# A graph layer on one core: where the first node numbers lie, and when the counts are taken

## The chip, the core and the metric

The kernel runs on one core of a Trainium2 chip. The metric is the device time of one execution in microseconds; the median of three runs is given. The engines have short names in all that follows: PE is TensorE (matmuls; PEld are its weight loads), DVE is VectorE, ACT is ScalarE, POOL is GpSimd, SP is SyncE. SBUF is the on-chip memory that all engines and DMAs reach; PSUM is the memory that PE writes its results to.

## The reference

There are 6250 nodes with 64 features and 206250 edges with 64 features each. Cut to what matters:

```python
msg = concatenate([x[dst], edge_attr], axis=1)        # 128 wide, one row per edge
h = relu(msg @ W1a.T + b1a) @ W1b.T + b1b             # the edge MLP, 128 hidden
sums, counts = segment_sum(h, src), segment_sum(ones, src)   # by the node src
agg = sums / maximum(counts, 1)
z = relu(concatenate([x, agg]) @ W2a.T + b2a) @ W2b.T + b2b  # the node MLP
y = concatenate([z, x]) @ Wr.T + br
out = layernorm(x + y)
```

The edges come sorted by dst. They have to be summed by src, which is in no order.

## The kernel before, in words

The host pads the edges and sends them in 124 blocks of 13 tiles of 128 edges (1664 edges a block). The blocks are taken in a fixed scattered order. A second, general path runs only where the data breaks the fast path's assumptions; it does not run here. All line numbers are those of the profile.

For each block k, the fast path does these steps.

- **Loads** (`group`, L1148 to L1170): SP issues the edge features of the block, transposed, and what names the dst nodes. Since the edges are sorted by dst, a block only meets 64 neighbouring nodes, its window. The first 8 blocks (NEAR) load their dst list and the 64 nodes; later ones load ready-made places in the window and rows of a table.
- **Columns** (`columns`, L1172): a one-hot of each edge's node within its window, so that one matmul handles both the edge and its node. For the first 8 blocks DVE makes it at L1184, comparing the dst list with `near_f`, which holds the window's node number for each of 64 partitions. For later blocks ACT makes it, in two passes (L1179, L1181).
- **Window** (`window`, L1189): for the first 8 blocks, a matmul (L1192) of the 64 nodes with the first layer's weights, and a copy by ACT (L1193) into `mv`, the weights of that block.
- **First layer** (`hidden`, L1199): 13 tiles, one matmul each in two passes (L1206), in groups of 4, 3, 3 and 3 that share a PSUM tile; ACT applies the relu (L1209) into the block's row tile `orow`, of which there are five.
- **Bins and counts**: src divided by 128 gives an edge's bin (49 of them). `carried` (L943) copies the running count of the block before into a first column (ACT, L956 or L959; DVE, L952, in the first blocks). `bins_of` (L915) makes one-hots by bin (L930) and scans them (L936), on DVE. `counts_of` (L963) turns them into each edge's rank in its bin with matmuls over partitions (L972, L973, L975), into the one PSUM tile `cnt`. `slots` (L978) reads `cnt` on DVE (L993 and, through `quads`, up to L1059) and writes the row index of every edge. Since there is one `cnt`, the counts of a block wait until the slots of the block before have read it.
- **Joins** (blocks 5 to 103): six or three of the tiles are added up by node into groups of four rows before they are written (marks by DVE at L1092, matmuls at L1115).
- **Scatter** (L1211): POOL issues one indirect DMA for each tile that is left (L1245) and for each joined group (L1217): 1306 in all. They write rows into tables in DRAM, sorted by bin. Some of them are told to wait for first-layer tiles, joins or sums of the block two places later.
- **Sums**: rows of bins that are full are read back (SP), DVE makes one-hots of their nodes (L1333), PE adds them up (L1352) and DVE or ACT adds the result to `part`.

Behind the last block come the sums of what is left and the node MLP with the norm (L1626 to L1690).

What sets the order: PE, ACT, DVE and SP run their instructions in the order in which the program writes them (a manual schedule). POOL's order is set by the framework's scheduler, which takes the instructions that are ready first by its own planning. Each engine takes its instructions strictly in order and waits on semaphores.

The main loop (L1501) prepares ahead: iteration k runs the first layer of block k, the counts and slots of block k + 1, the columns, the carried column and the scan of block k + 2, and the loads of block k + 3. Ahead of the loop (L1494 to L1500), block 0's window matmul, carried column, scan, counts, columns and slots run in the order written there.

`near_f` is 8 columns of `cnt` itself, in a PSUM bank that the counts also use: `cnt[:, 1, 448 : 456]`.

Of the kernel before, what the change touches and what calls it, by code (L numbers as in the profile page):

```python
# [8 lines left out]
F32 = mybir.dt.float32  # L9
# [8 lines left out]
P = 128  # L18
# [434 lines left out]
NEAR = 8  # L453
# [29 lines left out]
def fast_path(  # L483
# [61 lines left out]
    def joined(k):  # L545
        if not JOIN_FROM <= k < JOIN_TO:
            return 0
        return 2 if TWICE_FROM <= k < TWICE_TO else 1

    def direct(k):  # L550
        return BLK - JOIN * joined(k)
# [98 lines left out]
    const = ctx.enter_context(tc.tile_pool(name="fconst", bufs=1))  # L650
# [91 lines left out]
    with (  # L742
# [80 lines left out]
        def starts_at(joints):  # L823


            if joints:
                d = BLK - JOIN * joints
                nc.vector.memset(words, 1.0 + 0x3F80 * 2.0**-23)
                v = words.rearrange("p (b t) -> p b t", t=TJ)
                for c in (0, d + 1, TJ, TJ + d + 1):  # L830
                    if c % 2 == 0:
                        nc.vector.memset(v[:, :, c // 2], 1.0)
                    else:
                        nc.vector.memset(v.bitcast(I32)[:, :, c // 2], 0x3F80)
            else:
                v = words[:, : HALF * T]
                nc.vector.memset(v, 1.0 + 0x3F80 * 2.0**-23)
                nc.vector.memset(v.rearrange("p (b t) -> p b t", t=T // 2)[:, :, 0], 1.0)
# [9 lines left out]
        bins(0, HEAD)  # L848

        cnt = slpp.tile([P, 2, 512], F32, name="cnt_ps")  # L850
        near_f = cnt[:, 1, 448 : 448 + NEAR]
        z_ps = steady[:, P + 2 + HALF * TJ :][:, : 2 * JOIN]
        of_first = cnt[:, :, HALF * TJ : HALF * TJ + HALF]
        assert T % 2 == 0 and TJ % 2 == 1
# [60 lines left out]
        def bins_of(k):  # L915


            ep_ = epoch_of[k]
            c0 = k * BLK
            oh = ohs.pop(k)  # L920
            if joined(k) != joined(k - 1):
                starts_at(joined(k))
            t = TJ if joined(k) else T
            had = slp.tile([P, 2 * HALF * t], BF16, name="had", padded_shape=[P, 2 * HALF * TJ])
            by_bin = oh.rearrange("p (b t) -> p b t", t=t)
            d = direct(k)
            for t0, c, n in ((1, c0 + BLK - d, d), (d + 2, c0, BLK - d)):
                if n == 0:
                    continue
                nc.vector.tensor_tensor(  # L930
                    by_bin[:, :, t0 : t0 + n],
                    ramp[:, : 2 * HALF, None].to_broadcast([P, 2 * HALF, n]),
                    hi[:, None, c : c + n].to_broadcast([P, 2 * HALF, n]),
                    op=ALU.is_equal,
                )
            nc.vector.tensor_tensor_scan(had, on[:, : 2 * HALF * t], oh, 0.0, op0=ALU.mult, op1=ALU.add)  # L936
            oh, had = (v.rearrange("p (b t) -> p b t", t=t) for v in (oh, had))
            hads[k] = had
            return oh, had
# [3 lines left out]
        def carried(k):  # L943


            t, d = (TJ if joined(k) else T), direct(k)
            oh = ohs[k] = slp.tile([P, 2 * HALF * t], BF16, name="bins", padded_shape=[P, 2 * HALF * TJ])
            by_bin = oh.rearrange("p (b t) -> p b t", t=t)
            if k == epoch_of[k].first:
                nc.vector.memset(by_bin[:, :, 0], 0.0)  # L950
            elif k < JOIN_FROM:
                nc.vector.tensor_tensor(  # L952
                    by_bin[:, :, 0], hads[k - 1][:, :, BLK], ramp[:, 1:2].to_broadcast([P, 2 * HALF]), op=ALU.mult
                )
            elif joined(k) and joined(k - 1) == joined(k):
                nc.scalar.copy(by_bin[:, :, 0 : d + 2 : d + 1], hads[k - 1][:, :, d : d + 2])  # L956
                return
            else:
                nc.scalar.copy(by_bin[:, :, 0], hads[k - 1][:, :, direct(k - 1)])  # L959
            if joined(k):  # L960
                nc.scalar.copy(by_bin[:, :, d + 1], none_b)

        def counts_of(k, oh, had):  # L963
            t = oh.shape[2]

            ps = cnt
            for i in range(2):
                v = ps[:, i, : HALF * t].rearrange("p (b t) -> p b t", t=t)  # L970
                b = slice(i * HALF, (i + 1) * HALF)
                nc.tensor.matmul(v, one_w, had[:, b, :], start=True, stop=False)  # L972
                nc.tensor.matmul(v[:, :, : t - 1], before_w, oh[:, b, 1:], start=False, stop=True)  # L973
                if joined(k) == 2:
                    nc.tensor.matmul(of_first[:, i, :], one_w, had[:, b, direct(k) + 1 + JOIN], start=True, stop=True)  # L975
            return ps
# [171 lines left out]
        def group(g):  # L1148

            rhs = rhss[g % EDGES]  # L1150
            if g < NEAR:
                all_of = dst[g * NG * P : (g + 1) * NG * P].rearrange("(o e) -> o e", o=1)
                s = nc.sync.dma_start(rhs[D:, :].bitcast(I32), all_of.to_broadcast([WIN, NG * P]))
                edges(g)
                with tc.issue_after(s.ins):
                    w = nc.sync.value_load(win_i[0:1, g : g + 1], min_val=0, max_val=N - WIN)
                nc.sync.dma_start(near[:D, g, :], xT[:, bass.ds(w, WIN)])
                return rhs, None, mv[g % MV]
            edges(g)

            half = NG * P // 2
            rel = rhs[D:, :].bitcast(BF16).rearrange("p (h e) -> p h e", h=2)[:, :, half:]
            s = nc.sync.dma_start(
                rel, relt[g : g + 1, :].rearrange("o (h e) -> o h e", h=2).to_broadcast([WIN, 2, half])
            )
            with tc.issue_after(s.ins):
                w = nc.sync.value_load(win_i[0:1, g : g + 1], min_val=0, max_val=N - WIN)
            m = mv[g % MV]
            nc.sync.dma_start(m[D:, :], ytab[bass.ds(w, WIN), :])
            return rhs, rel, m  # L1170

        def columns(g, part_of=0):  # L1172


            rhs, rel, _ = made[g]
            if g >= NEAR:
                of_win = rhs[D:, :].rearrange("p (h e) -> p h e", h=2)
                if part_of == 0:
                    nc.scalar.activation(of_win, rel, AF.Square, bias=from_win[D:, :])  # L1179
                else:  # L1180
                    nc.scalar.activation(rhs[D:, :], rhs[D:, :], AF.Relu, bias=ones[D:, :1], scale=-1.0)  # L1181
                return
            if part_of == 0:
                nc.vector.tensor_tensor(  # L1184
                    rhs[D:, :], rhs[D:, :].bitcast(I32), near_f[D:, g : g + 1].to_broadcast([WIN, NG * P]),
                    op=ALU.is_equal,
                )

        def window(g):  # L1189

            ps = hp.tile([P, H], F32, name="h_ps")
            nc.tensor.matmul(ps[D:, :], near[: D + 1, g, :], w1x_t, start=True, stop=True)  # L1192
            nc.scalar.copy(mv[g % MV][D:, :], ps[D:, :])  # L1193
# [5 lines left out]
        def hidden(k, parts):  # L1199
            orow = orows[k % ROWS]  # L1200
            rhs, _, m = made[k]
            for k0, n in parts:
                ps = hp.tile([P, SUB, H], F32, name="h_ps")
                for j in range(n):
                    c = k0 + j
                    done[k, c] = nc.tensor.matmul(  # L1206
                        ps[:, j, :], rhs[:, c * P : (c + 1) * P], m, start=True, stop=True
                    ).ins.name
                nc.scalar.activation(orow[:, k0 : k0 + n, :H], ps[:, :n, :], AF.Relu)  # L1209
# [283 lines left out]
        )  # L1493
        for g in range(3):  # L1494
            made[g] = group(g)
        window(0)
        carried(0)
        counts = counts_of(0, *bins_of(0))
        columns(0)
        slots(0, counts)  # L1500
        for k, ep_ in enumerate(epoch_of):  # L1501
# [15 lines left out]
            if k == 0:  # L1517
                hidden(k, ((0, 4), (4, 3), (7, 3), (10, 3)))
                window(1)
                columns(1)  # L1520
                carried(1)
                ahead = bins_of(1)
            if k + 1 < NGR:
                counts = counts_of(k + 1, *ahead)
            if k + 2 < NGR:
                carried(k + 2)
            if k > 0:
                hidden(k, ((0, 4), (4, 3), (7, 3)))
            if k + 2 < NEAR:
                window(k + 2)  # L1530
            if k == NEAR - 6:
# [255 lines left out]
```

## Time and profile before

| | us |
|---|---|
| three runs | 1740.62, 1749.65, 1750.46 |
| their median | 1749.65 |
| the profiled execution | 1742.9 |
| its span, first to last instruction | 1741.1 |
| PE busy | 1495.1 (86%) |
| DVE busy | 1451.1 (83%) |
| POOL busy | 1255.2 (72%) |
| ACT busy | 900.1 (52%) |
| mean granted PE clock | 0.953 |

A row of a group reads: line, engine, operation, what it writes and reads, number of instructions; then busy time in us and the mean of one in ns; then the engine's idle time just before these instructions, and what ended most of it. "issue" is idle time in which the engine waited for nothing that the profile shows. A row of the timeline reads: start and length in us, engine and line; equal neighbours are merged (x26), and the brackets tell the idle time before. SPq, ACTq and POOLq are the sequencers, which issue DMAs. All durations come from one profiled execution.

### The profile page before, as it was taken

Reading aid. Unit: us, or ns where it says so; the run is one execution under the profiler, and the core shown is the slowest. Engines: PE = TensorE matmul, PEld = TensorE weight load, DVE = VectorE, ACT = ScalarE, POOL = GpSimd, SP = SyncE. Lnnn points to the kernel's source line nnn. Section 1 sums busy time; section 2 is a strip of 40 time slices with the busy share of each in tenths; the row PEclk is TensorE's granted clock in tenths of the full one; section 3 lists DMA queues with packets and bytes.
Section 4 is the critical chain, followed back from the end, with each engine's and each line's share of the span. In section 5 each row is a group of like instructions: output and inputs, shape, how many; then the busy total and the mean of one; then the engine's idle time right before and its main releaser. Section 6 shows DMA issues by size and latency. Waiting matters only on the chain. (4 is left out here: it accounts for less than half of the span.)

```text
span 1741.1 us, 36105 instructions
## 1 busy us (share of the span) xinstructions
PE 1495.1 (86%) x12229; PEld 1426.3 (82%) x12229; DVE 1451.1 (83%) x3408; ACT 900.1 (52%) x1797; POOL 1255.2 (72%) x1323
## 2 busy tenths in 40 slices
PE   5668888888888888776899999989889999999987
PEld 4568878788878787766798999889889898999976
DVE  8489999999999899766788988989877676888777
ACT  2257777666766666554555555545443333443026
POOL 5777777777777777777777777777777777777720
PEclk9789999989999999978999999999999999999998
DMA  8878888856666565558799999879788888999971
GB/s 185 217 242 273 275 271 271 278 175 190 189 189 189 169 200 169 163 167 238 213 267 271 288 286 276 272 233 269 221 248 255 247 239 252 273 322 298 334 231 47
DMA packets 216190, 408.89 MB, mean 235 GB/s; under 512 B 43265, under 2 KB 122740, under 8 KB 215868
## 3 DMA queue, kind: packets, MB, share of 16 engines
q1 hardware_dynamic: 127770, 230.22, 47.1%
q0 software_dynamic: 49136, 117.56, 20.7%
q10 hardware_dynamic: 39090, 58.69, 10.6%
q8 instruction: 100, 1.64, 0.4%
q14 instruction: 94, 0.77, 0.1%
HBM read 228.29 MB, written 178.01 MB: 233 GB/s over the span
## 5 line engine op out<-in xcount | busy, mean ns | idle before, releaser
L1245 POOL DMA_INDIRECT rows<-orow,rowidx x1153 | 1105.8, 959 | 368.6 <-issue 216.0
L1352 PE MATMUL h_ps<-rt,oh 128*128 128x129 f32 x4202 | 511.4, 280 | 44.8 <-DVE oh L1333 17.4
L1352 PEld LDWEIGHTS h_ps<-rt,oh 128*128 128x128 f32 x4202 | 495.1, 196 | 50.6 <-issue 21.6
L1206 PE MATMUL h_ps<-mv,rhs 128*128 128x128 f32 x3224 | 416.2, 285 | 26.3 <-ACT orow L1209 18.4
L1206 PEld LDWEIGHTS h_ps<-mv,rhs 128*128 128x128 f32 x3224 | 397.5, 200 | 38.8 <-ACT orow L1209 21.3
L1209 ACT ACTIVATE orow<-h_ps 128x512 f32<-128x512 f32 x496 | 255.1, 538 | 302.8 <-PE h_ps L1206 296.2
L1333 DVE TENSOR_TENSOR oh<-ramp,rt 128x512 f32<-128x512 f32 (+4 forms) x466 | 332.3, 752 | 26.9 <-DMA rt<-rows 22.3
L1115 PE MATMUL h_ps<-orow,shared 128*128 128x130 f32 (+1 forms) x2376 | 302.6, 285 | 38.9 <-ACT orow L1209 32.6
L1115 PEld LDWEIGHTS h_ps<-orow,shared 128*128 128x128 f32 x2376 | 291.7, 200 | 43.3 <-ACT orow L1209 37.0
L936 DVE TENSOR_TENSOR_SCAN had<-ramp,bins 128x750 bf16<-128x750 bf16 (+1 forms) x124 | 210.6, 1699 | 99.0 <-ACT bins L956 90.3
L1179 ACT ACTIVATE rhs<-rhs,from_win 64x1664 f32<-64x1664 bf16 x116 | 194.6, 1677 | 2.9
L1181 ACT ACTIVATE rhs<-rhs,ones 64x1664 f32<-64x1664 f32 x116 | 194.6, 1677 | 2.9
L1092 DVE TENSOR_TENSOR shared<-quad_ramp,ramp 128x1536 f32<-128x1536 f32 x99 | 173.4, 1751 | 11.0 <-PE h_ps L1115 4.8
L1507 ACT CAST orow<-lo 128x13 f32<-128x13 bf16 x124 | 26.5, 214 | 292.9 <-DMA rows<-orow,rowidx 256.9
L972 PE MATMUL cnt_ps<-had,one_w 128*128 128x375 bf16 (+1 forms) x248 | 81.8, 332 | 85.5 <-DVE at_q L1059 74.0
L1115 PE MATMUL h_ps<-orow,oh 128*128 128x130 f32 (+1 forms) x1296 | 154.3, 275 | 0.0
L1115 PEld LDWEIGHTS h_ps<-orow,oh 128*128 128x128 f32 x1296 | 149.8, 190 | 0.0
L1119 ACT COPY shared<-h_ps 128x260 f32<-128x260 f32 x168 | 62.2, 378 | 109.2 <-PE h_ps L1115 51.1
L930 DVE TENSOR_TENSOR bins<-ramp,hi 128x300 bf16<-128x300 f32 (+2 forms) x223 | 113.7, 548 | 0.3
L1409 DVE TENSOR_TENSOR part<-part,h_ps 128x387 f32<-128x387 f32 (+2 forms) x207 | 89.9, 435 | 21.2 <-PE h_ps L1352 20.4
L973 PEld LDWEIGHTS <-before_w 128*128 128x128 bf16 x248 | 25.5, 103 | 99.9 <-issue 94.3
L1217 POOL DMA_INDIRECT quads<-shared,qidx x84 | 80.6, 960 | 25.6 <-issue 10.7
(161 smaller groups left out, 1291.9 us busy)
## 6 DMA issues: line engine op xcount, KB each, us to landing
rhs<-in_edgeT SPq DMA_DIRECT2D x124, 416.0 KB
rt<-rows SPq DMA_DIRECT2D x106, 390.0 KB
rt<-rows SPq DMA_DIRECT2D x145, 260.0 KB
rt<-quads SPq DMA_DIRECT2D x97, 260.0 KB
rhs<-relt SPq DMA_DIRECT2D x116, 208.0 KB
rows<-padrow ACTq DMA_DIRECT2D x12, 1560.0 KB
rows<-orow,rowidx POOLq DMA_INDIRECT x1153
rt<-rows SPq DMA_DIRECT2D x48, 325.0 KB
```

The source lines that it names most:

```text
L930: nc.vector.tensor_tensor(by_bin[:, :, t0 : t0 + n], ramp[:, : 2 * HALF, None].to_broadcast([P, 2 * HALF, n]), hi[:, None, c : c + n].to_b ...
L936: nc.vector.tensor_tensor_scan(had, on[:, : 2 * HALF * t], oh, 0.0, op0=ALU.mult, op1=ALU.add)
L1092: nc.vector.tensor_tensor(m, quad_ramp.rearrange("p g q -> p (g q)")[:, None, :].to_broadcast([P, JOIN, QUAD * P]), z_ps[:, i * JOIN : (i ...
L1115: done[k, f"join{i}"] = nc.tensor.matmul(ps[:, j, :w], m[:, t, (g0 + j) * P : (g0 + j + 1) * P], orow[:, i * JOIN + t, :w], start=t == 0, ...
L1179: nc.scalar.activation(of_win, rel, AF.Square, bias=from_win[D:, :])
L1181: nc.scalar.activation(rhs[D:, :], rhs[D:, :], AF.Relu, bias=ones[D:, :1], scale=-1.0)
L1206: done[k, c] = nc.tensor.matmul(ps[:, j, :], rhs[:, c * P : (c + 1) * P], m, start=True, stop=True).ins.name
L1209: nc.scalar.activation(orow[:, k0 : k0 + n, :H], ps[:, :n, :], AF.Relu)
L1245: s = nc.gpsimd.indirect_dma_start(out=ep_.rows, out_offset=bass.IndirectOffsetOnAxis(ap=rowidx[:, k % RING * BLK + j : k % RING * BLK + j ...
L1333: nc.vector.tensor_tensor(res[:, at_tile : at_tile + nb * n, :], ramp[:, None, :].to_broadcast([P, nb * n, P]), node[:, :, None].to_broadc ...
L1352: m = nc.tensor.matmul(of_bin(b), oh[:, at_tile, :], rt[:, j * n + t, : H + 1], start=t0 + t == st.lo[b], stop=t0 + t == st.hi[b] - 1,)
L1409: nc.vector.tensor_add(to, to, g.ps[:, : g.nb, :])
```

## The change

Three things. First, `near_f` becomes a small tile of its own in SBUF, instead of columns of the counts' PSUM tile. Second, ahead of the loop the counts of block 0 come before the window matmul of block 0 on PE, and before the window's copy on ACT. Third, in every iteration from block 1 on, the first group of four first-layer tiles of block k (matmuls and relu) comes ahead of the counts of block k + 1 and ahead of the carried column of block k + 2; the next two groups stay where they were.

```diff
-        near_f = cnt[:, 1, 448 : 448 + NEAR]
+        near_f = const.tile([P, NEAR], F32, name="near_f")
...
         for g in range(3):
             made[g] = group(g)
-        window(0)
         carried(0)
         counts = counts_of(0, *bins_of(0))
+        window(0)
         columns(0)
         slots(0, counts)
...
+            if k > 0:
+                hidden(k, ((0, 4),))
             if k + 1 < NGR:
                 counts = counts_of(k + 1, *ahead)
             if k + 2 < NGR:
                 carried(k + 2)
             if k > 0:
-                hidden(k, ((0, 4), (4, 3), (7, 3)))
+                hidden(k, ((4, 3), (7, 3)))
             if k + 2 < NEAR:
                 window(k + 2)
```

## The prediction

> **What bounds the kernel now.** I read four views in this order: engine totals, the windows by stage, the groups, and the timeline of the first 20 us. The totals (busy time, share of the span, instructions) come first.
>
> ```profile
> span 1741.1 us, 36105 instructions
> PE 1495.1 (86%) x12229; PEld 1426.3 (82%) x12229; DVE 1451.1 (83%) x3408; ACT 900.1 (52%) x1797; POOL 1255.2 (72%) x1323
> ```
>
> By these shares TensorE looks like the bound, and POOL like a bystander. The windows view, cut at the first and the last scatter, says otherwise (columns: length, then busy time and instruction count of each engine, granted clock, DMA share, GB/s).
>
> ```profile
> 0.00:17.10 17.10, 5.49 (x23) 4.30 (x24) 11.28 (x29) 2.84 (x6) 2.51 (x17) 1.00 0.86 179
> 17.10:1671.10 1654.00, 1436.70 (x11828) 1375.64 (x11828) 1389.85 (x3237) 858.26 (x1610) 1252.68 (x1306) 0.96 0.81 240
> 1671.10:1741.10 70.00, 52.91 (x383) 46.32 (x381) 49.95 (x144) 39.02 (x182) 0.00 (x0) 0.88 0.41 120
> ```
>
> All 1306 scatters lie in the middle stage. 1654.0 / 1306 = 1.266 us for each. Is that a fixed pace, or POOL waiting for others? The groups and the last scatters answer it.
>
> ```profile
> L1245 POOL DMA_INDIRECT rows<-orow,rowidx x1153 | 1105.8, 959 | 368.6 <-issue 216.0 <-DMA rows<-orow,rowidx 45.2 <-PE h_ps L1206 22.7
> L1217 POOL DMA_INDIRECT quads<-shared,qidx x84 | 80.6, 960 | 25.6 <-issue 10.7 <-DMA rows<-orow,rowidx 4.0 <-DVE oh L1333 1.8
> L1217 POOL DMA_INDIRECT quads<-rt,qidx x69 | 66.3, 961 | 21.0 <-issue 11.9 <-DMA rows<-orow,rowidx 2.1 <-DVE hit_q L1139 1.5
> ...
> 1668.84 0.96 POOL L1245 DMA_INDIRECT rows<-orow,rowidx  x1 [0.30 <-issue]
> 1670.10 0.96 POOL L1245 DMA_INDIRECT rows<-orow,rowidx  x1 [0.30 <-issue]
> ```
>
> Three groups, one duration (959 to 961 ns), and 0.30 us before each even where nothing is waited for. 1305 gaps of 0.30 are 391.5 us. The idle time of the groups is 368.6 + 25.6 + 21.0 = 415.2, of which 13.95 lie before the first scatter (below), so 401.3: some 10 us at most are true waiting in 1654. The hundreds in between say the same, where TensorE idles and where it doesn't:
>
> ```profile
> 400.00:500.00 100.00, 86.04 (x730) 82.00 (x729) 95.02 (x254) 68.37 (x137) 75.91 (x80) 0.98 0.63 190
> ...
> 700.00:800.00 100.00, 65.98 (x455) 61.83 (x454) 66.80 (x179) 51.30 (x98) 75.75 (x80) 0.83 0.59 167
> ...
> 1500.00:1600.00 100.00, 100.00 (x888) 98.83 (x888) 86.62 (x132) 43.72 (x58) 75.89 (x80) 1.00 1.00 313
> ```
>
> Eighty scatters start in each, whatever PE and DVE do. So the span is **17.1 us to the first scatter + 1654.0 of scatters back to back + 70.0 behind the last**. An edit counts only if it moves the first scatter, stalls POOL, or touches the tail.
>
> **The change part by part.** *The start.* These rows of the timeline (start, length, engine, line; in brackets the idle time before and what ended it) carry it:
>
> ```profile
> 2.16 0.58 SPq L1153 DMA_DIRECT2D rhs<-in_dst_o  x1
> 4.76 0.50 SPq L1157 DMA_DIRECT2D rt<-in_xT  x1
> 6.47 1.62 DVE L936 TENSOR_TENSOR_SCAN had<-ramp,bins 128x700 bf16<-128x700 bf16 x1
> 9.59 0.66 PE L1192 MATMUL h_ps<-w1x_t,rt 65*64 65x128 f32 x2 [9.59 <-DMA rt<-in_xT]
> 10.18 0.47 PE L972 MATMUL cnt_ps<-had,one_w 128*128 128x350 bf16 x1
> 10.28 0.26 ACT L1193 COPY mv<-h_ps 64x128 f32<-64x128 f32 x1 [5.91 <-PE h_ps L1192]
> 11.03 0.50 PE L973 MATMUL cnt_ps<-bins,before_w 128*128 128x325 bf16 x1
> 11.56 1.89 DVE L1184 TENSOR_TENSOR rhs<-rhs,cnt_ps 64x1664 f32<-64x1664 int32 x1 [3.47 <-PE cnt_ps L973]
> 13.55 5.37 PE L1206 MATMUL h_ps<-mv,rhs 128*128 128x128 f32 x26 [2.03 <-issue]
> 14.59 0.17 DVE L1000 SCALAR_TENSOR_TENSOR rowidx<-row,bin_at 128x13 int32<-128x13 f32 x1
> 15.63 0.60 ACT L1209 ACTIVATE orow<-h_ps 128x512 f32<-128x512 f32 x1 [4.85 <-PE h_ps L1206]
> 17.10 1.13 POOL L1245 DMA_INDIRECT rows<-orow,rowidx  x1 [13.95 <-DVE rhs L1184]
> ```
>
> Now: the one-hots of block 0 (L1184) read near_f out of the tile of the counts and wait 3.47 us for the last count; the first layer starts 0.1 us after they end at 13.45; the first scatter is issued 17.10 - 13.55 = 3.55 us later. After the change near_f is a tile of its own, and in the compiled order the first L1184 waits only for its load. It can start at the scan's end, 6.47 + 1.62 = 8.09, and end at 9.98. The counts run from 8.1: four matmuls that now take 10.18 to 11.53 end at about 9.5. The window matmul still waits for its load until 9.59 and its copy ends at 10.54. So the first layer starts at about 10.6, not 13.55. The new row indices end 9.98 + (14.76 - 13.45) = 11.3, early enough. **First scatter: 10.6 + 3.55 = 14.15, 2.95 us earlier.** The second L1184, which the page names as releaser, ends by 13.2 and doesn't hold it.
>
> The one unknown is when the list that L1184 reads has landed. It was issued at 2.16, 2.6 us ahead of a load that was there at 9.59. If it lands at 8.09 or before, the gain is 2.95. If at 9.59, L1184 ends at 11.48, the first layer starts at 11.58, and the gain is 1.97. I take 2.95: the earlier issue is the nearer row.
>
> L1184 itself changes an operand from PSUM to SBUF. No row has that operation with both operands in SBUF, so I compare two other tensor-tensor rows of one size:
>
> ```profile
> L1679 DVE TENSOR_TENSOR normed<-y,rstd 128x192 f32<-128x192 f32 (+1 forms) x17 | 6.0, 350 | 0.5
> L1665 DVE TENSOR_TENSOR y<-h_ps,xr 128x192 f32<-128x192 f32 (+1 forms) x17 | 5.8, 341 | 0.4 <-PE h_ps L1663 0.4
> ```
>
> SBUF with SBUF took 350 ns, PSUM with SBUF 341: 3% either way, 0.06 us on 1.89, eight times. Nothing.
>
> *The counts behind four tiles.* TensorE's wait ahead of the counts goes:
>
> ```profile
> L972 PE MATMUL cnt_ps<-had,one_w 128*128 128x375 bf16 (+1 forms) x248 | 81.8, 332 | 85.5 <-DVE at_q L1059 74.0 <-DVE row L993 7.8 <-DVE early L998 3.4
> ```
>
> That is 85.2 us over 123 blocks, 0.69 each, which four tiles fill: 8 passes of 3.15 / 26 = 0.12 us make 0.97 us. Since POOL sets the pace it is worth 0 at the end. What it may cost is seen in a block of the stage where DVE is fullest:
>
> ```profile
> 296.50 0.30 DVE L1059 TENSOR_TENSOR at_q<-cnt_ps,second 128x150 f32<-128x150 f32 x1
> 296.85 0.32 PE L972 MATMUL cnt_ps<-had,one_w 128*128 128x375 bf16 x1 [1.77 <-DVE at_q L1059]
> 297.57 3.15 PE L1206 MATMUL h_ps<-mv,rhs 128*128 128x128 f32 x26
> 299.17 0.60 ACT L956 COPY bins<-had 128x100 bf16<-128x100 bf16 x1
> 299.36 0.84 ACT L1209 ACTIVATE orow<-h_ps 128x512 f32<-128x512 f32 x1
> 301.97 1.72 DVE L936 TENSOR_TENSOR_SCAN had<-ramp,bins 128x750 bf16<-128x750 bf16 x1
> 304.48 0.51 DVE L993 TENSOR_REDUCE row<-cnt_ps 128x7 f32<-128x350 f32 x1
> 307.47 0.30 DVE L1059 TENSOR_TENSOR at_q<-cnt_ps,second 128x150 f32<-128x150 f32 x1
> ```
>
> Two things come later. The counts come up to 0.97 us later where PE wasn't waiting; their reader (L993) starts at 304.48, 6.7 us after they end at 297.75. The carried column (L956) now queues on ACT behind the activation of the four tiles, 0.60 us as at 15.63; the scan that needs it starts 2.2 us after its end at 299.77. Both are covered. Without the cover the price would be 0.97 + 0.60 = 1.57 us of DVE a block. Behind the copy on ACT stand the other activations, whose work is the same. No DMA is moved in any queue's order; SP's loads for later blocks wait for first-layer tiles of earlier ones, which come no later.
>
> *Stalls and the tail.* The only long wait between scatters, and the longest issue on ACT's queue, lie in the stage that loads and writes most:
>
> ```profile
> 90.91 0.97 POOL L1245 DMA_INDIRECT rows<-orow,rowidx  x1 [2.52 <-issue]
> 51.85 17.74 ACTq L807 DMA_DIRECT2D ytab<-part  x1
> ```
>
> If transfers there keep their own time while POOL comes 2.95 us earlier, POOL waits up to 2.95 more. If they move along, as I take it since their issues follow the same engines, nothing is lost. Between 0 and 2.95 of the gain are at stake. The tail follows the last scatter and stays 70.0.
>
> **Sum:** 14.15 + 1654.0 + 70.0 = 1738.15 of span. The profiled execution took 1742.9, 1.8 more than its span, so 1739.9 by its own measure, 2.95 less. That execution lies 6.75 below the median of the three runs shown (1740.62, 1749.65, 1750.46), which spread over 9.8 us. Against the median: 1749.65 - 2.95 = **1746.7**.
>
> **The rivals.**
> *A. TensorE was the bound after all.* Then 85.2 us of waits go: 1664.5. For it: 86% busy, and the chain that ended last is mostly PE lines. Against: x80 in every hundred, the one with PE at 65.98 too. 0.02.
>
> *B. The one-hots hold up POOL.* L1184 gets two SBUF operands while scatters read their indices from SBUF. Seven of the eight (the first runs before any scatter) could each stop POOL for 1.89 us: +13.2 - 2.95 = +10.3, 1759.9. Other operations already have two SBUF operands beside scatters (minimum, median, maximum in ns):
>
> ```profile
> L1048 DVE TENSOR_TENSOR cumq<-n_i,cumq x153: 210/211/282, 76.5 to 1288.1; 128x50 f32<-128x50 int32 x153
> L1245 POOL DMA_INDIRECT rows<-orow,rowidx x1153: 952/958/1647, 17.1 to 1670.1; - x193
> ```
>
> 153 of them against a POOL that is busy three quarters of the time: none waited out a scatter of 0.96, and the median scatter is within 6 ns of the shortest. 0.07.
> The Trainium skill states the rule in "SBUF — State Buffer", section "Who interferes with whom": a DVE instruction with two SBUF inputs contends with a GpSimd instruction that reads SBUF, and the loser "fully blocks". By it the sum would be this rival's; the L1048 row (282 ns at most) speaks against it for these scatters.
>
> *C. Slower: the scan starves POOL.* ACT's new order makes the carried column so late that DVE waits in each of the 54 blocks with two joins. DVE needs 307.47 - 296.50 = 10.97 us a block, nine scatters 11.40: 0.43 to spare. With the whole 1.57 on DVE's path, 1.14 x 54 = 62 us: 1808. It decides only when the column is over 2.2 us late. 0.04.
>
> *D. The head start is lost,* to the busy stage at 50 to 90 us or because L1184 still waits: +0 to +2 instead of -2.95, 1749.65. 0.20.
>
> **How the numbers follow.** The forecast has 0.65, A 0.02, B 0.07, C 0.04, D 0.20, and 0.02 is left for what I don't see. Forecast, B and D lie within 1% of 1749.65 (17.5 us), about what a measurement of this kernel can tell from no change: 0.93 with half of the unseen. Faster by over 1%: 0.02. Slower: 0.05. The range goes from the fastest run less the gain and a little of the waits (1740.62 - 2.95 - 1.7 = 1736) to the slowest run without a gain and 2.5 of B's first holds (1753); outside are A, C and most of B.
>
> **What the new profile would show.** Right: first L1184 near 8.1 with no wait for cnt_ps, first scatter near 14.2, last near 1667, eighty scatters per hundred, L972's wait for at_q nearly gone, and PE's idle time showing elsewhere. Wrong: first scatter at 15 or later (the list landed late), scatters over 1 us beside L1184 (B), gaps over 0.4 between scatters in blocks 8 to 61 with longer waits of L936 for L956 (C).

## The result, and the profile after

The changed kernel takes **1752.05 us** (median of 22 runs, 1749.56 to 1758.66); the kernel before, run beside it, 1748.32 us (22 runs, 1740.62 to 1751.54). The ratio on record is 1.0031, 95% interval 1.0023 to 1.0040: 5.4 us slower (4.0 to 7.0 us). It is not the quotient of the two medians, which would be 1.0021, or 3.7 us; nor are the ratios below. The forecast was 2.95 us faster. The range held the time, but the sign was wrong.

The windows view of the kernel after, cut at its own first and last scatter as it was cut before (length, busy time and count of each engine, granted clock, DMA share, GB/s):

```profile
0.00:14.06 14.06, 5.54 (x24) 4.38 (x25) 11.66 (x29) 2.85 (x6) 2.52 (x17) 1.00 0.83 175
14.06:1679.66 1665.60, 1454.95 (x11787) 1392.48 (x11787) 1383.33 (x3231) 848.36 (x1610) 1261.76 (x1306) 0.94 0.82 239
1679.66:1750.30 70.64, 55.87 (x423) 49.12 (x421) 53.64 (x151) 39.00 (x182) 0.00 (x1) 0.93 0.41 119
```

Against the three stages before (17.10, 1654.00, 70.00) the head is 3.04 us shorter, the stage of the scatters 11.6 us longer, and the tail 0.6 us longer. These two executions lie 9.2 us of span apart; the runs, 5.4. The execution profiled before (1742.9 us) is 5.4 us below the median of its 22 runs, the one profiled after (1752.09) is at its median. The head did what the prediction said. The timeline of the kernel after, cut to the lines that lead to the first scatter:

```profile
8.15 1.89 DVE L1184 TENSOR_TENSOR rhs<-rhs,near_f 64x1664 f32<-64x1664 int32 x1
8.17 0.45 PE L972 MATMUL cnt_ps<-had,one_w 128*128 128x350 bf16 x1 [8.17 <-DVE had L936]
...
10.17 0.26 ACT L1193 COPY mv<-h_ps 64x128 f32<-64x128 f32 x1 [5.79 <-PE h_ps L1192]
...
10.48 4.68 PE L1206 MATMUL h_ps<-mv,rhs 128*128 128x128 f32 x26 [0.35 <-ACT mv L1193]
...
14.06 1.13 POOL L1245 DMA_INDIRECT rows<-orow,rowidx  x1 [10.90 <-ACT orow L1209]
```

L1184 no longer waits for the counts, the counts run beside it, and the first layer starts at 10.48 instead of 13.55. The loss is in the middle stage. The view by tile (minimum, median, maximum in ns) shows where to look:

```profile
L1184 DVE TENSOR_TENSOR rhs<-rhs,near_f x8: 1889/1890/1945, 8.1 to 80.0; 64x1664 f32<-64x1664 int32 x8
L1245 POOL DMA_INDIRECT rows<-orow,rowidx x1153: 955/962/2271, 14.1 to 1678.7; - x193
```

The longest scatter was 1647 ns before (what held that one is said further below) and is 2271 now. The timeline of the kernel after, cut to L1184 and the scatters around three of its runs:

```profile
15.50 0.96 POOL L1245 DMA_INDIRECT rows<-orow,rowidx  x1 [0.30 <-issue]
...
16.31 1.89 DVE L1184 TENSOR_TENSOR rhs<-rhs,near_f 64x1664 f32<-64x1664 int32 x1
...
16.76 2.27 POOL L1245 DMA_INDIRECT rows<-orow,rowidx  x1 [0.30 <-issue]
...
23.11 1.95 DVE L1184 TENSOR_TENSOR rhs<-rhs,near_f 64x1664 f32<-64x1664 int32 x1
23.14 0.96 POOL L1245 DMA_INDIRECT rows<-orow,rowidx  x1 [0.30 <-issue]
...
24.40 1.49 POOL L1245 DMA_INDIRECT rows<-orow,rowidx  x1 [0.30 <-issue]
...
79.98 1.89 DVE L1184 TENSOR_TENSOR rhs<-rhs,near_f 64x1664 f32<-64x1664 int32 x1
...
80.69 2.02 POOL L1245 DMA_INDIRECT rows<-orow,rowidx  x1 [0.30 <-issue]
```

A scatter that starts inside an L1184 (not in its first hundredths of a us, as at 23.14) is held until 0.83 us after that L1184 ends: 16.31 + 1.89 = 18.20, and the scatter ends at 16.76 + 2.27 = 19.03. For the second, 25.06 and 25.89. A free scatter takes 0.96, so the held one stood still from about 0.13 us after its start. Of the eight L1184, two run before any scatter (8.15 and 11.27; before the change too, at 11.56 and 14.79); each of the other six holds one. The held scatters take 2.27, 1.49, 1.54, 1.76, 1.65 and 2.02 us, together 10.73 instead of 6 x 0.96 = 5.76: **4.97 us of holds.** Before, with the list in PSUM, no scatter was held beside an L1184. The timeline of the kernel before, the same lines:

```profile
27.05 1.89 DVE L1184 TENSOR_TENSOR rhs<-rhs,cnt_ps 64x1664 f32<-64x1664 int32 x1
...
27.38 0.96 POOL L1245 DMA_INDIRECT rows<-orow,rowidx  x1 [0.30 <-DMA rows<-orow,rowidx]
28.64 0.95 POOL L1245 DMA_INDIRECT rows<-orow,rowidx  x1 [0.30 <-issue]
```

The whole of the 11.6 us can be split by the groups of POOL. The groups of the kernel after:

```profile
L1245 POOL DMA_INDIRECT rows<-orow,rowidx x1153 | 1114.5, 967 | 364.5 <-issue 214.2 <-DMA rows<-orow,rowidx 45.0 <-PE h_ps L1206 21.3
L1217 POOL DMA_INDIRECT quads<-shared,qidx x84 | 80.8, 962 | 26.4 <-issue 10.0 <-DMA rows<-orow,rowidx 4.7 <-DVE oh L1333 2.7
L1217 POOL DMA_INDIRECT quads<-rt,qidx x69 | 66.4, 962 | 23.9 <-issue 9.5 <-DMA rows<-orow,rowidx 4.0 <-DVE oh L1092 2.0
```

Busy time rose by 8.7 + 0.2 + 0.1 = 9.0 us: the 4.97 of the holds, and 4.0 that are spread over all 1306 scatters, 3 ns each (the shortest is 955 instead of 952, the median 962 instead of 958). Idle time between scatters rose from 401.3 to 364.5 + 26.4 + 23.9 - 10.9 = 403.9, 2.6 us.

### The profile page after: what moved, and what is told of

It is laid out like the page before. It is cut to its first block, busy times and chain, and to the rows that moved or that the text cites. A ratio compares the mean times of both kernels' runs of the same rounds, so it can differ in the third digit from the quotient of the medians.

```text
span 1750.3 us, 36161 instructions
## 1 busy us (share of the span) xinstructions
PE 1516.4 (87%) x12229; PEld 1446.0 (83%) x12229; DVE 1448.6 (83%) x3408; ACT 890.2 (51%) x1797; POOL 1264.3 (72%) x1323
## 4 chain that ended last, share of the span: by engine, by line
PE 45%; DMA 19%; DVE 18%; issue 7%; ACT 5%; POOL 4%; ACTq 1%; SPq 1%; DVEq 0%; POOLq 0%
PE h_ps L1352 22%; DMA rows<-orow,rowidx 15%; PE h_ps L1206 9%; PE h_ps L1115 8%; POOL rows L1245 3%; DVE had L936 3%; DVE shared L1092 3%; DVE oh L1092 2%; DMA quads<-shared,qidx 2%; ACT rhs L1179 2%; ACT orow L1209 1%; PE h_ps L801 1%; DVE row L993 1%; DVE bins L930 1%; DMA rt<-rows 1%
## 5 line engine op out<-in xcount | busy, mean ns | idle before, releaser
L1245 POOL DMA_INDIRECT rows<-orow,rowidx x1153 | 1114.5, 967 | 364.5 <-issue 214.2
L1352 PE MATMUL h_ps<-rt,oh 128*128 128x129 f32 x4202 | 514.6, 281 | 45.6 <-DVE oh L1333 14.5
L1352 PEld LDWEIGHTS h_ps<-rt,oh 128*128 128x128 f32 x4202 | 496.8, 196 | 52.4 <-issue 15.1
L1206 PE MATMUL h_ps<-mv,rhs 128*128 128x128 f32 x3224 | 432.3, 284 | 24.2 <-ACT of_q L1121 13.9
L1206 PEld LDWEIGHTS h_ps<-mv,rhs 128*128 128x128 f32 x3224 | 404.0, 198 | 35.6 <-ACT of_q L1121 14.4
L1209 ACT ACTIVATE orow<-h_ps 128x512 f32<-128x512 f32 x496 | 262.3, 543 | 280.1 <-PE h_ps L1206 274.9
L1115 PE MATMUL h_ps<-orow,shared 128*128 128x130 f32 (+1 forms) x2376 | 317.2, 294 | 65.1 <-ACT orow L1209 59.0
L1115 PEld LDWEIGHTS h_ps<-orow,shared 128*128 128x128 f32 x2376 | 304.6, 207 | 72.3 <-ACT orow L1209 66.2
L1115 PE MATMUL h_ps<-orow,oh 128*128 128x130 f32 (+1 forms) x1296 | 153.8, 274 | 0.0
L1115 PEld LDWEIGHTS h_ps<-orow,oh 128*128 128x128 f32 x1296 | 149.4, 190 | 0.0
L972 PE MATMUL cnt_ps<-had,one_w 128*128 128x375 bf16 (+1 forms) x248 | 81.6, 331 | 58.2 <-DVE at_q L1059 42.5
L1217 POOL DMA_INDIRECT quads<-shared,qidx x84 | 80.8, 962 | 26.4 <-issue 10.0
L1092 DVE TENSOR_TENSOR oh<-quad_ramp,ramp 128x1536 f32<-128x1536 f32 x54 | 94.3, 1747 | 0.0
```

What stands on the lines that cost most here:

```text
L1092: nc.vector.tensor_tensor(m, quad_ramp.rearrange("p g q -> p (g q)")[:, None, :].to_broadcast([P, JOIN, QUAD * P]), z_ps[:, i * JOIN : (i ...
L1115: done[k, f"join{i}"] = nc.tensor.matmul(ps[:, j, :w], m[:, t, (g0 + j) * P : (g0 + j + 1) * P], orow[:, i * JOIN + t, :w], start=t == 0, ...
L1206: done[k, c] = nc.tensor.matmul(ps[:, j, :], rhs[:, c * P : (c + 1) * P], m, start=True, stop=True).ins.name
L1245: s = nc.gpsimd.indirect_dma_start(out=ep_.rows, out_offset=bass.IndirectOffsetOnAxis(ap=rowidx[:, k % RING * BLK + j : k % RING * BLK + j ...
L1352: m = nc.tensor.matmul(of_bin(b), oh[:, at_tile, :], rt[:, j * n + t, : H + 1], start=t0 + t == st.lo[b], stop=t0 + t == st.hi[b] - 1,)
```

## The experiments

**Theory:** the scatters set the pace; the start gains 3 us; the six one-hots, which now read both operands from SBUF, hold scatters up by 5 us; the four tiles moved ahead of the counts cost nothing. **Rivals:** the moved tiles cost the time (later counts, other waits for landings); or the list in SBUF is harmless and the long scatters are chance.

Three edits make up the change. "List" is the tile of its own in SBUF, "counts first" the window behind block 0's counts, "tiles" the four tiles ahead of later counts.

```diff
# list
-        near_f = cnt[:, 1, 448 : 448 + NEAR]
+        near_f = const.tile([P, NEAR], F32, name="near_f")
# counts first
-        window(0)
         carried(0)
         counts = counts_of(0, *bins_of(0))
+        window(0)
# tiles
+            if k > 0:
+                hidden(k, ((0, 4),))
...
-                hidden(k, ((0, 4), (4, 3), (7, 3)))
+                hidden(k, ((4, 3), (7, 3)))
```

One thing is needed to read the numbers: runs e1 to e14 fell on chips where the kernel before itself takes 2346 to 2372 us at a granted clock of about 0.84, and e15 to e18 on one where it takes 1745.61 us.

### The parts alone, on a chip whose scatters wait: e1 to e4

e1: list alone. e2: counts first alone. e3: tiles alone. e4: counts first and tiles, list left in PSUM.

> near_f as a tile in SBUF, and nothing else. Theory H (holds: a scatter that starts while L1184 runs with two SBUF operands is stretched, 5.0 us in all for six of them in the changed kernel): the first scatter comes near 15.1, since the counts of block 0 still follow the window matmul and the first layer follows them; five or six scatters of 1.5 to 2.3 us beside L1184; time +3 us on the kernel before (+0.15 to +0.3%). Theory T (the moved tiles and what they do to POOL's order cost the time, the holds are made good later): -2 us (-0.1%), held scatters or not.

> The first counts ahead of the window matmul, near_f in PSUM, tiles where they were. Counts from 8.1 to 9.5, L1184 from 9.5, first layer at about 11.5, first scatter near 15.05, 2.05 us earlier. No scatter beside L1184 is longer than 1 us. H and T both: -2 us (-0.1%). If it is 0 or slower, the head start itself is lost behind the first scatters, and neither theory is enough.

> The first four tiles ahead of the counts in each block, near_f in PSUM, the start as before. First scatter at 17.1. H: 0 (within 0.1%), no held scatters. T: +3 to +5 us (+0.2 to +0.3%), from waits between scatters in blocks 9 to 30 (130 to 360 us), where the changed kernel has seven of 0.4 to 1.4 us and the kernel before two.

> The whole change except that near_f stays in PSUM. First scatter near 15.05. H: -2 us (-0.1%), no held scatters. T: +1 to +3 us.

Against 2345.83 us of the kernel before: e1 2346.77, ratio 1.0012 (0.9994 to 1.0031); e2 2339.50, 0.9984 (0.9962 to 1.0007); e3 2313.47, 0.9870 (0.9844 to 0.9895); e4 2309.85, 0.9859 (0.9833 to 0.9885). The tiles, priced at 0 in the forecast, are worth 1.3 to 1.4% here. The reason is that the bound is another one. The largest group of POOL in e1:

```profile
L1245 POOL DMA_INDIRECT rows<-orow,rowidx x1153 | 1110.2, 963 | 883.6 <-ACT orow L1209 312.7 <-issue 270.3 <-remote 92.3
```

The two largest groups of PE in e1:

```profile
L1352 PE MATMUL h_ps<-rt,oh 128*128 128x129 f32 x4202 | 677.5, 314 | 244.7 <-issue 225.9 <-DVE oh L1333 5.8 <-DVE qidx L1144 5.0
L1206 PE MATMUL h_ps<-mv,rhs 128*128 128x128 f32 x3224 | 507.2, 312 | 105.4 <-issue 101.5 <-ACT shared L1119 1.5 <-ACT part L1407 0.3
```

The first of these in the kernel before, on the chip of the prediction:

```profile
L1352 PE MATMUL h_ps<-rt,oh 128*128 128x129 f32 x4202 | 511.4, 280 | 44.8 <-DVE oh L1333 17.4 <-issue 13.9 <-ACT of_q L1121 5.6
```

And one hundred of the windows of e1:

```profile
400.00:500.00 100.00, 81.06 (x592) 73.27 (x591) 76.69 (x216) 55.90 (x109) 62.28 (x65) 0.91 0.57 176
```

POOL waits 883.6 us ahead of its scatters, mostly for what the first layer makes, and starts 65 of them in the hundred instead of 80. TensorE stands still 225.9 us ahead of L1352 for nothing that the profile shows, where the kernel before, on the other chip, stood 13.9. In the chain of work that ended last, PE has 66% of the span in e1 and 25% in the kernel before. So here the chain runs through TensorE, and an edit that moves its work counts. Which wait the 1.3% come out of these runs don't settle. It isn't the wait ahead of the counts (L972) that the forecast looked at: there it comes to 21.1 us in e1 and 27.5 in e3.

On the one-hots: e1 holds six scatters (1.72, 1.49, 1.54, 1.67, 2.44 and 1.51 us), and e2 to e4, whose list is in PSUM, none beside a one-hot. The list in SBUF is the cause of the holds, and not the moves. What the holds cost the end can't be seen here, since POOL waits anyway.

### Repeats, another form of the one-hots, the change itself: e5 to e10

e5, e6 and e7 repeat e1, e4 and e3. e8 is the whole change with L1184 written as a compare with one scalar for each partition, with a sum over the row that nobody reads:

```diff
-                nc.vector.tensor_tensor(
-                    rhs[D:, :], rhs[D:, :].bitcast(I32), near_f[D:, g : g + 1].to_broadcast([WIN, NG * P]),
-                    op=ALU.is_equal,
+                nc.vector.tensor_scalar(
+                    rhs[D:, :], rhs[D:, :].bitcast(I32), near_f[D:, g : g + 1], None,
+                    op0=ALU.is_equal, op1=ALU.add, accum_out=hits[D:, :],
```

e9 repeats e4 once more, beside e10, the changed kernel itself.

> The edit of e1 once more, for a chip on which scatters run back to back. H (holds): first scatter near 14.8, 5 us of holds beside L1184, so +3 us (+0.15 to +0.3%). T (moved tiles): -2 us (-0.1%). Where PE sets the end, as in e1: 0 (within 0.2%).

> The edit of e4 once more: the whole change but near_f in PSUM. Scatters back to back: H -2 us (-0.1%), T +1 to +3 us. Where PE sets the end, as in e4: -1.2 to -1.7%.

> The edit of e3 once more: only the four tiles ahead of the counts. Scatters back to back: H 0 (within 0.1%); T +3 to +5 us (+0.2 to +0.3%) with waits between scatters at 130 to 360 us. Where PE sets the end, as in e3: -1.0 to -1.6%.

> The whole change, but L1184 takes near_f's column as a scalar operand (the form that also writes a sum), so that it reads one tensor in SBUF. H: no scatter beside it over 1.1 us, first scatter near 14.1, -3 us (-0.15%) where scatters run back to back, 5 us less than the changed kernel. T: +1 to +3 us, as the tiles are moved too. If scatters are still stretched beside it, the second tensor operand is not what holds them.

> The edit of e4 and e6 again, since on both chips so far the scatters did not run back to back (229 waits between them, 540 us, against 4 and 3 us in the profile before). Where they do: H (holds alone made the change slower) -2 us (-0.1%), no scatter over 1.1 us beside L1184; T (the moved tiles cost) +1 to +3 us. Where they don't: -1.2 to -1.7% as in e4 and e6.

> The changed kernel itself, beside e9 on one chip. Where scatters run back to back: +0.2 to +0.4% as on record, 5 us of it (0.3%) in six held scatters, so by H 0.35 to 0.45% above e9, by T level with e9 within 0.2%. Where they don't: the gain of e9 within 0.3%, since held scatters in the first 90 us cost nothing when POOL waits for PE later.

Against 2371.79 us: e5 2363.63, 0.9975 (0.9946 to 1.0004); e6 2335.22, 0.9852 (0.9823 to 0.9882); e7 2344.04, 0.9897 (0.9868 to 0.9926); e8 2339.03, 0.9881 (0.9843 to 0.9919). Against 2368.69 us: e9 2339.84, 0.9879 (0.9844 to 0.9914); e10 2338.99, 0.9874 (0.9835 to 0.9913).

The change that costs 0.31% beside the first series is 1.3% faster here (e10). With six held scatters (e10) or none (e8, e9) the gain is the same within its intervals of 0.35 to 0.4%. These are wider than the 5 us of the holds, which are 0.2%, so that a hold costs nothing where POOL waits anyway is to be expected and not shown. The timeline of e10 shows the same hold at the same place as the kernel after, at another speed of the chip:

```profile
16.32 1.89 DVE L1184 TENSOR_TENSOR rhs<-rhs,near_f 64x1664 f32<-64x1664 int32 x1
...
16.75 2.29 POOL L1245 DMA_INDIRECT rows<-orow,rowidx  x1 [0.30 <-issue]
```

It isn't chance. e10 also shows its free scatters at 952 ns (shortest) and 958 ns (median), as in the kernel before: the 3 ns more on each scatter in the profile after do not belong to the changed program as such. They come and go without regard to the edit: e5 and e7 have 955 and 962 ns, while e1 and e3, with the same edits, have 952 and 958 to 959.

### An attempt to make POOL the pace on such a chip: e11 to e14

These four leave out work, so their outputs are not the reference's: of the matmuls that sum rows (L1352) only the last tile of each bin and step is kept, and of those of the joins (L1115) about half; the flag that chooses the general path is held at 0. e11 is the kernel before so lightened, e12 the kernel after, e13 counts first and tiles, e14 tiles alone.

```diff
-                    for t in range(JOIN):
+                    ts = range(JOIN) if g0 + j == 0 else range(JOIN - 1, JOIN)
+                    for t in ts:
...
+                        if t0 + t == st.hi[b] - 1:
```

> The kernel before with less matmul work: of the summing matmuls only the last tile of each bin and step, of the joins' only what the places need, and the flag for the general path is held at 0. Scatters back to back (under 30 us of waits between them), span about 17 + 1660 + a shorter tail of some 60: near 1735 us. It is the base for the three below.

> The changed kernel with the same matmuls left out. First scatter at 14.1, six held scatters, 5.0 us. H (holds and head start are all): +2 us on e11. T (moved tiles cost too): +4 to +7 us on e11.

> Both moves, near_f in PSUM, the same matmuls left out. First scatter at 15.1, no held scatter. H: -2 us on e11, 4 us below e12. T: 0 to +4 us on e11.

> Only the moved tiles, near_f in PSUM, the same matmuls left out. First scatter at 17.1. H: 0 on e11 (within 1.5 us). T: +2 to +5 us, with more or longer waits between scatters than in e11.

They took 2125.11, 2110.34, 2116.95 and 2119.64 us, not 1735: the lightening didn't make POOL the pace. The windows of e12:

```profile
700.00:800.00 100.00, 74.40 (x429) 66.73 (x429) 79.48 (x221) 55.80 (x111) 64.29 (x67) 0.77 0.54 159
1500.00:1600.00 100.00, 56.60 (x312) 50.65 (x310) 59.35 (x129) 33.91 (x57) 62.08 (x65) 0.72 0.64 186
```

Still 65 to 67 scatters a hundred, with the clock granted even lower. They say nothing on the holds' price. A miss.

### The parts on a chip whose scatters run back to back: e15 to e18

e15 is the list alone, e16 the tiles alone, e17 counts first and tiles, e18 the kernel of e8.

> Only the list of first nodes lies in SBUF; counts and tiles stay where they were. Theory (on a chip whose scatters run back to back the held scatters eat the head start): first scatter some 2.3 us earlier than in the kernel before, six scatters of 1.5 to 2.4 us worth about 5, so +2 to +3 us, ratio 1.001 to 1.002. If the remaining 2 to 5 us of the changed kernel's loss also come from the list: 1.003. On a chip where TensorE is fed slowly (the kernel before near 2350): 0.9975 to 1.001, holds there and worth nothing.

> Only the later counts stand behind four tiles. Theory: no scatter beside a one-hot over 1 us, first scatter near 17.1. Back to back: 1.000 if the move is free there, up to 1.002 to 1.003 if the moved tiles make scatters wait longer for the landing of earlier ones. TensorE fed slowly: 0.987 to 0.990.

> Both moves, the list stays in PSUM. Theory: first scatter 15.1, no held scatter; back to back 2 us faster, ratio 0.999; if the moved tiles cost the remaining loss, 1.001 to 1.002. TensorE fed slowly: 0.985 to 0.988.

> The whole change, with the one-hots made by a compare against a per-partition scalar instead of two tensors in SBUF. Theory: first scatter 14.1, no held scatter; back to back 3 us faster than the kernel before, ratio 0.998, and 8 us faster than the changed kernel. If the holds were not the cause: 1.003 as the changed kernel. TensorE fed slowly: 0.985 to 0.990, like the change.

Against 1745.61 us (35 runs; each of the four had 12):

| | us | ratio (95%) | that is, us | first scatter | stage of scatters |
|---|---|---|---|---|---|
| e15 list | 1747.13 | 1.0014 (1.0002 to 1.0025) | +2.4 (+0.3 to +4.4) | 14.65 | 1656.85 |
| e16 tiles | 1745.45 | 1.0010 (0.9999 to 1.0022) | +1.7 (-0.2 to +3.8) | 17.37 | 1652.06 |
| e17 counts first + tiles | 1743.06 | 0.9998 (0.9989 to 1.0008) | -0.3 (-1.9 to +1.4) | 15.06 | 1654.38 |
| e18 all, scalar form | 1743.09 | 0.9990 (0.9979 to 1.0002) | -1.7 (-3.7 to +0.3) | 14.45 | 1653.79 |

By the medians alone the four would stand at +1.5, -0.2, -2.5 and -2.5 us. The last two columns are from the windows of each. Those of e15:

```profile
0.00:14.65 14.65, 5.15 (x23) 4.42 (x24) 11.06 (x29) 2.83 (x6) 2.51 (x17) 1.00 0.82 178
14.65:1671.50 1656.85, 1435.79 (x11799) 1372.17 (x11799) 1387.21 (x3233) 855.93 (x1610) 1257.87 (x1306) 0.96 0.82 240
```

Those of e18:

```profile
0.00:14.45 14.45, 5.56 (x22) 4.38 (x23) 11.74 (x31) 2.83 (x6) 2.51 (x17) 1.00 0.83 170
14.45:1668.24 1653.79, 1442.62 (x11753) 1381.22 (x11753) 1380.99 (x3230) 858.15 (x1610) 1253.07 (x1306) 0.95 0.83 240
```

**e15** has the first scatter 17.10 - 14.65 = 2.45 us earlier and six held scatters (1.71, 1.49, 1.55, 2.52, 2.31 and 1.50 us, 5.32 us over 6 x 0.96): 2.87 us slower by this sum, 2.4 measured. The list alone makes the kernel slower although it starts sooner. Its timeline:

```profile
35.42 1.89 DVE L1184 TENSOR_TENSOR rhs<-rhs,near_f 64x1664 f32<-64x1664 int32 x1
...
35.63 2.52 POOL L1245 DMA_INDIRECT rows<-orow,rowidx  x1 [0.30 <-issue]
```

**e18** differs from the changed kernel in the form of L1184 alone. It starts 2.65 us earlier than the kernel before, and no scatter is held beside a one-hot. Its timeline, cut to L1185 (the one-hot) and the scatters:

```profile
16.74 1.95 DVE L1185 TENSOR_SCALAR_CACHE_REDUCE rhs<-rhs,near_f 64x1664 f32<-64x1664 int32 x1
...
17.15 0.96 POOL L1246 DMA_INDIRECT rows<-orow,rowidx  x1 [0.30 <-issue]
18.41 0.96 POOL L1246 DMA_INDIRECT rows<-orow,rowidx  x1 [0.30 <-issue]
```

And its scatters in the view by tile:

```profile
L1246 POOL DMA_INDIRECT rows<-orow,rowidx x1153: 952/958/1645, 14.5 to 1667.3; - x193
```

The scatter at 17.15 runs wholly beside the one-hot and takes 0.96. The ratio goes from 1.0031 to 0.9990 with this one line; the two intervals don't overlap. The difference is 0.41% (its interval, from the two half-widths 0.085% and 0.115% added as squares, is plus or minus 0.14%), so 7.2 us (4.7 to 9.6). The 4.97 us of the holds lie within that. The two ratios come from different series of runs, each against the kernel before in its own; which chip the first was taken on isn't on record.

**e16 and e17** test the rival of the moved tiles. In the profiles their stage of scatters isn't longer than the 1654.00 of before beyond 0.4 us; in the runs e16 is 1.7 us slower with an interval that reaches -0.2. A price of the tiles between 0 and some 4 us isn't excluded, but not shown.

e18 has the lowest ratio of the four. Where the scatters run back to back its gain isn't told from nothing (the interval reaches 1.0002); on a chip whose scatters wait it gains 1.2% (e8).

## Why the prediction was wrong, step by step

**The bound: right, on that chip.** 1653.79 / 1306 = 1.266 us for a scatter in e18, as before; PE idles where it may. On other chips the same program has another bound. Rival A (TensorE the bound, the counts' wait goes) was given 0.02 for the profile shown, and there it was rightly small. On the chips of e1 to e10 its first half holds, and the versions with the tiles moved gain 1.0 to 1.5%, not 4.9%. Its second half does not: the counts' wait is small there even without the tiles (21.1 us in e1).

**The start: right.** First layer forecast at 10.6, seen at 10.48; first scatter 14.15 and 14.06.

**L1184's new operand: the step that failed.** The forecast priced the change of operand by two rows of DVE's own duration, "3% either way", "Nothing". DVE's duration indeed stayed (1890 ns, 1891 before). The price fell on POOL: 4.97 us. Rival B said just that and was given 0.07, on a reading of the L1048 row that doesn't hold. It took "none waited out a scatter of 0.96" as evidence of no conflict. But an L1048 lasts 0.21 us, and a held scatter stands still only from about 0.13 us after its start. So beside an L1048 it can be held for 0.08 us at most, and in most meetings for nothing: this operation could not stretch any scatter far enough to be seen in a median or a maximum. And the 282 ns, quoted as speaking against the conflict, were the conflict. The timeline of the kernel before, cut to L1048 and the scatters:

```profile
743.06 0.28 DVE L1048 TENSOR_TENSOR cumq<-n_i,cumq 128x50 f32<-128x50 int32 x1
743.10 0.96 POOL L1217 DMA_INDIRECT quads<-rt,qidx  x1 [0.30 <-DVE off_q L1045]
```

This L1048 began with a scatter beside it and was the one that waited, 0.07 us over its 0.21. The like is seen in the profile after, where the L1184 at 23.11 takes 1.95 and the scatter at 23.14 its plain 0.96. A conflict whose loser is the short operation is a sign of what a long one will do to the other side.

The other side stood in the same fence: the longest scatter of 1647 ns. The kernel before has three scatters (78.20, 103.55 and 104.94, the longest) that are stretched beside DVE operations of 0.93 us and more, and the first shows the same 0.83 us. The timeline of the kernel before, cut to that operation and the scatter:

```profile
77.58 1.14 DVE L789 TENSOR_SCALAR rt<-rt,at_f 124x1664 bf16<-124x1664 int32 x1
...
78.20 1.35 POOL L1245 DMA_INDIRECT rows<-orow,rowidx  x1 [0.31 <-issue]
```

L789 ends at 78.72 and the scatter at 79.55. This operation reads one tensor and a scalar for each partition, so two tensors in SBUF are not the only form that holds a scatter. Asking what stretched these three would have shown that a DVE operation of 1 us can stop POOL.

That the range held the time all the same is luck: its upper end was the slowest of three runs and 2.5 us allowed for rival B's first holds, not the forecast's own mechanism.

Rival B's price was an upper bound, 7 x 1.89 = 13.2 us; the measured sum is 4.97. Two of the eight L1184 run ahead of the first scatter where rival B counted one, and each of the rest costs only what is left of it when the scatter wants its operands: 0.53 to 1.31 us.

The Trainium skill's rule, in "SBUF — State Buffer", section "Who interferes with whom" (a DVE instruction with two SBUF inputs contends with a GpSimd instruction that reads SBUF), was set against the L1048 row, and the row was misread. The trace agrees with the rule: six scatters held, none in e2 to e4 or e16 and e17 with the list in PSUM. Among the operations that can take the ports which DVE shares with GpSimd, the same section names tensor_scalar, but not the form that also writes out its accumulator; the trace agrees on both, with L789 above and with the scatter of 0.96 beside the one-hot of e18. The section also infers that a tensor-tensor operation doesn't stall descriptor generation; the scatters here, whose indices lie in SBUF, are held by one, and these runs don't show which part of the scatter stands still.

**The four tiles: no price was shown, but the wait did not go.** The forecast put 0.97 us of tiles into L972's wait and expected the wait for at_q to be "nearly gone". The group in the kernel after:

```profile
L972 PE MATMUL cnt_ps<-had,one_w 128*128 128x375 bf16 (+1 forms) x248 | 81.6, 331 | 58.2 <-DVE at_q L1059 42.5 <-DVE had L936 8.6 <-DVE row L993 3.8
```

In e16, with the tiles alone:

```profile
L972 PE MATMUL cnt_ps<-had,one_w 128*128 128x375 bf16 (+1 forms) x248 | 82.1, 333 | 87.3 <-DVE at_q L1059 75.7 <-DVE row L993 6.5 <-DVE early L998 3.3
```

With the tiles alone it is 87.3 us, where it was 85.5; 93.7 in e17 and e18. So the 58.2 of the kernel after are not the work of the tiles alone. The timeline of e16 shows one block:

```profile
294.76 1.05 PE L1206 MATMUL h_ps<-mv,rhs 128*128 128x128 f32 x8
...
297.52 0.32 PE L972 MATMUL cnt_ps<-had,one_w 128*128 128x375 bf16 x1 [1.71 <-DVE at_q L1059]
```

The four tiles are done before the wait and don't fill it. In this block PE reaches the tiles earlier and then stands as long as before (1.71 us, 1.77 before); for the other blocks this isn't shown. Rival C's 62 us did not come: all idle time between scatters rose by 2.6 us.

**The busy stage and the rest.** The 2.52 us wait at 90.91 is gone in the kernel after, and there are others. The timeline of the kernel after:

```profile
58.10 0.96 POOL L1245 DMA_INDIRECT rows<-orow,rowidx  x1 [1.49 <-PE h_ps L1206]
```

Such waits come to 2.6 us more in that execution, and in e15 (its three groups have 363.8, 25.6 and 21.0, with 11.5 ahead of the first scatter) to 398.9, 2.4 us less than the 401.3 of before. From one profile to the next they differ by about what was at stake.

**What stays open.** Start and holds make -3.04 + 4.97 = +1.9 us; the runs say +5.4 (4.0 to 7.0). The 2.1 to 5.1 us between are not settled, and either of two causes would do for most of it. One is the pace of the scatters: the 3 ns more on each make 4.0 us in the profile after, but e1, e3, e5 and e7 show that they don't follow the edit, and whether all 22 runs had them isn't known, since one was profiled. The other is the tiles (e16: -0.2 to 3.8): e17 starts 2.04 us earlier and gains 0.3, e18 starts 2.65 earlier and gains 1.7, which points the same way, but by the medians both gain 2.5 and nothing is missing. The changed kernel itself was not run beside e15 to e18, where its holds would have been priced against e18 directly.

## What to carry to other kernels

When an operand moves from PSUM to SBUF, ask for the cost on every engine that reads SBUF meanwhile, and not only for the duration of the operation itself; a long operation with two SBUF operands beside a POOL that sets the pace costs what is left of it, once for each. A form with one tensor operand isn't free of it by that alone (L789 held a scatter, the form with the sum in e18 did not), so look for the held scatter in the trace. To rule a conflict out by a row, first ask what that row could show at most: a 0.21 us operation cannot show a hold of 1.3 us, and the few of its runs that took a little longer were the evidence. Where a kernel has several engines near the bound, the same edit may help on one chip and hurt on another, so look at which wait ends last on the chip at hand.

## What the runs showed of the hardware that was not expected

The conflict has two sides: a scatter that starts within 0.04 us after the DVE operation wins and costs it up to 0.07 us (L1048 at 743.06). One that starts 0.05 us after it already loses: in the kernel before, the scatter at 596.56 beside an L1045 of 0.21 us from 596.51, which has two operands in SBUF too, takes 1.01. Beside L1184 the closest is 65.75 against 65.65 in e12, with 2.62 us. The loser stands until DVE's end and ends 0.83 us behind it, in all 35 held scatters of the kernel after and of e1, e5, e10, e12 and e15 (0.83 to 0.85). And the same kernel took 1745.61 us on one chip and 2346 to 2372 on others. Between e1, on one of those, and the profile before, the free scatters are the same (952 and 958 ns), and TensorE has idle time that no wait explains (225.9 us before L1352 against 13.9). Taking matmuls out (e11 to e14) brought the time to 2110 to 2125 us and the granted clock from 0.84 down to 0.75. What makes these chips differ is not shown.
